# Attention and two quantized convolutions on one core: the instructions in emitted order on every engine, and one kind of single PSUM bank

## The chip, the cores and the metric

The kernel runs on one core of a Trainium2 chip. The metric is the device time of one launch in microseconds: the median of three runs before the change is 3111.85 us (3110.21 to 3114.57). The profiled execution has a span of 3108.4 us, and TensorE was granted a mean clock of 0.981 in it.

In the profile PE is TensorE's matmuls, PEld its weight loads, DVE is VectorE, ACT is ScalarE, POOL is GpSimd, and SP is the engine that here only issues DMAs. Each of them takes its own stream of instructions.

## The reference, cut to what matters

```python
# x: (4, 128, 64, 64); 4 heads of 32 channels; 4096 positions in each image
x_norm = group_norm(x)                                  # 8 groups
q, k, v = split(einsum('oc,bchw->bohw', qkv_w, x_norm) + qkv_b)
attn = softmax(einsum('bhid,bhjd->bhij', q, k) * d ** -0.5)
out  = einsum('bhij,bhjd->bhid', attn, v)
x    = x + einsum('oc,bchw->bohw', proj_w, out) + proj_b
# then, with 3x3 weights quantized to 3 bits:
y = relu(batchnorm(conv3x3(x, wq1)))
y = batchnorm(conv3x3(y, wq2))
return relu(y + x)
```

Attention is most of the work: 4 images x 4 heads x 4096 x 4096 scores, each of which is exponentiated.

## The kernel before: the parts concerned

One **block** is one image and 512 query positions; there are 32 blocks, n = 0 to 31, 8 for each image. A block has 32 **steps**, kt = 0 to 31, one for each 128 key positions. A step needs two **pairs** of score matmuls (two heads each), two exponentials of 128x1024 on ACT, and four matmuls `acc` that weigh the values. The four `acc` matmuls use 32 columns of the array each, so that the four heads stand beside each other; the score matmuls use all 128 columns.

```python
pss = tc.tile_pool(name="pss", bufs=3, space=PSUM)   # 3 x 2 banks: a pair of scores
psa = tc.tile_pool(name="psa", bufs=1, space=PSUM)   # one bank for each kind
ppool = ...bufs=6      # exponentials of one step, 128 x 2048
stage, rpool = ...bufs=1

def scores(pair):                                    # two pairs are one step
    ...
    for i in range(2):
        nc.tensor.matmul(s[:, i, :], k[:, h, c0 : c0 + P], q[:, h, :], ...)
    nc.scalar.activation(pts[step][:, 2 * half : 2 * half + 2, :], s, AF.Exp, scale=SCALE)

def weights(step):
    if kt == 0:
        acc[n] = psa.tile([P, FB], F32, name=f"acc{n}", tag="acc")
    for h in range(HEADS):
        nc.tensor.matmul(acc[n][h * D : (h + 1) * D, :], v[...], pt[:, h, :], ...)
    if kt in MOVED:                # 0, 4, ... 24: this step's sum is made by a DMA that adds
        (kt == 0): nc.sync.dma_start(out=msum[n], in_=pt)
        (else):    nc.gpsimd.dma_start(out=msum[n], in_=pt, accum_op=ALU.add)
    elif kt == 2: nc.vector.tensor_tensor(rsum[n], pts[step - 1], pt, ALU.add)
    elif kt > 2:  nc.vector.tensor_tensor(rsum[n], rsum[n], pt, ALU.add)

run_scores(2)
while at["step"] < steps:
    for s, w in ((3, 1), (3, 2)):      # 3 pairs, 1 step; 3 pairs, 2 steps
        run_scores(s)
        run_weights(w)
```

So scores run two and a half steps ahead of the weighing. The rest of the work is dealt out between: `run_scores` ends with `side("q", kt)` and each step of `run_weights` with `side("a", kt)`, which call what the block's timetable holds up to that step.

```python
add(2, "a", before["total"])          # the previous block's sums: 8 matmuls `l`, then ACT copies to ls
add(4 + j, "", before["invert"](j))   # DVE, four times
add(8, "", before["weigh"]); add(10, "q", before["project"]); add(11, "", before["store"])

def chunk(b, j, kt, fs, loads):       # q, k, v of 512 positions of the next image
    add(kt, "", fs[0])                # ACT: xn <- x
    add(kt, "q", fs[1])               # PE:  pk <- xn
    add(kt + 1, "", fs[2])            # ACT: kh <- pk; DVE: kl <- pk, kh; two DMAs
    add(kt + 1, "q", fs[3])           # PE:  pq <- xn     (pk, pq, pv, l, po: one bank, tag "m")
    add(kt + 2, "", fs[4])            # ACT: qh <- pq; DVE: ql <- pq, qh; two DMAs
    add(kt + 2, "q", fs[5])           # PE:  pv <- xn
    add(kt + 3, "", fs[6])            # DVE: vst <- pv; a DMA
```

Image 0's chunks 3 to 7 are made in block 0. The 8 chunks of each next image are made in the blocks before it: two each in the third and fourth block of an image, one each in the fifth to the eighth. In the last image no chunk is left to make; 8 tasks that quantize the convolution weights on DVE are dealt out there from its second block on.

The convolutions follow, then the last stage:

```python
for b in range(B):
    for j in range(4):
        r = outs.tile([P, Q], F32, tag="r")                      # bufs=4
        nc.sync.dma_start(out=r, in_=y0[b][:, cs])
        y = outs.tile([P, Q], F32, tag="y")                      # bufs=4
        nc.vector.scalar_tensor_tensor(y, cv[b][:, cs], a2, r, ALU.mult, ALU.add)
        nc.scalar.activation(y, y, AF.Relu, bias=c2)
        nc.sync.dma_start(out=out[...][:, cs], in_=y)
```

The code is recorded once, in the order in which it is written; before the change a scheduler then chooses each engine's order from it, and puts one instruction before another where it expects it to be ready sooner.

Of the kernel before, what the change touches and what calls it, by code (L numbers as in the profile page):

```python
# [16 lines left out]
F32 = mybir.dt.float32  # L17
# [3 lines left out]
PSUM = bass.MemoryType.PSUM  # L21

P = 128
# [4 lines left out]
FB = 512  # L28
# [39 lines left out]
def _fast(tc, x, norm_w, norm_b, qkv_wt, qkv_b, proj_wt, proj_b,  # L68
          w1, alpha1, gamma1, beta1, w2, alpha2, gamma2, beta2, out, outer):
    flag = outer.enter_context(tc.tile_pool(name="flag", bufs=1))  # L70
    cnt = flag.tile([1, 1], I32, name="cnt")
    with ExitStack() as ctx:
        _fast_body(ctx, tc, x, norm_w, norm_b, qkv_wt, qkv_b, proj_wt, proj_b,
                   w1, alpha1, gamma1, beta1, w2, alpha2, gamma2, beta2, out, cnt)
    return tc.nc.values_load(cnt[0:1, 0:1], min_val=0, max_val=P)


def _fast_body(ctx, tc, x, norm_w, norm_b, qkv_wt, qkv_b, proj_wt, proj_b,
# [116 lines left out]
    dram = ctx.enter_context(tc.tile_pool(name="dram", bufs=1, space=bass.MemoryType.DRAM))  # L195
    kpool = ctx.enter_context(tc.tile_pool(name="kpool", bufs=NB + 1))
    pss = ctx.enter_context(tc.tile_pool(name="pss", bufs=3, space=PSUM))
    psa = ctx.enter_context(tc.tile_pool(name="psa", bufs=1, space=PSUM))
    y0 = [dram.tile([P, N], F32, name=f"y0_{b}") for b in range(B)]
    att = ExitStack()  # L200
    vpool = att.enter_context(tc.tile_pool(name="vpool", bufs=NB + 1))
# [9 lines left out]
    def f32(t):  # L211
        return t.bitcast(F32)
# [12 lines left out]
    def norm_parts(b, st):  # L225
        mv = small.tile([P, 2], F32, name=f"mv{b}", tag="mv")
        mean = small.tile([P, 1], F32, name=f"mean{b}", tag="mean")
        dv = small.tile([P, 1], F32, name=f"dv{b}", tag="dv")
        gm = {}


        def one():
            nc.vector.bn_aggr(mv, st.rearrange("p j s -> p (j s)"))
            gm[0] = psa.tile([P, FB], F32, name=f"gm{b}", tag="m")
            nc.tensor.matmul(gm[0][:, 0:1], gavg, mv[:, 0:1], start=True, stop=True)

        def two():
            nc.vector.tensor_copy(mean, gm[0][:, 0:1])
            nc.vector.tensor_tensor(dv, mv[:, 0:1], mean, ALU.subtract)
            nc.vector.tensor_tensor(dv, dv, dv, ALU.mult)  # L240
            nc.vector.tensor_tensor(dv, dv, mv[:, 1:2], ALU.add)

        def three():
            gm[1] = psa.tile([P, FB], F32, name=f"gv{b}", tag="m")
            nc.tensor.matmul(gm[1][:, 0:1], gavg, dv, start=True, stop=True)

        def four():
            r = rsqrt_eps(gm[1][:, 0:1], f"gr{b}")
            a = small.tile([P, 1], F32, name=f"ga{b}", tag="ga")
            nc.vector.tensor_tensor(a, r, nw, ALU.mult)  # L250
            c = small.tile([P, 1], F32, name=f"gc{b}", tag="gc")
            nc.vector.tensor_tensor(c, mean, a, ALU.mult)
            nc.vector.tensor_tensor(c, nb, c, ALU.subtract)
            norm[b] = a, c

        return one, two, three, four


# [4 lines left out]
    def project_parts(b, j, xin, wide=False):  # L263
        xn = xpool.tile([P, FB], F32, name=f"xn{b}_{j}", tag="x")
        kq[b, j] = dram.tile([5, P, FB], F32, name=f"kq{b}_{j}")
        ps = {}

        def bank(what):
            if wide:
                t = pss.tile([P, 2, FB], F32, name=f"p{what}{b}_{j}", tag="s")  # L270
                return t[:, 0, :]
            return psa.tile([P, FB], F32, name=f"p{what}{b}_{j}", tag="m")

        def normalize():
            a, c = norm[b]
            nc.scalar.activation(xn, xin(), AF.Identity, bias=c, scale=a)

        def mm(what, o):
            ps[what] = bank(what)
            nc.tensor.matmul(ps[what], wqkv[:, o : o + P], xn, start=True, stop=True)  # L280

        def parts(what, bias, slot):
            hi = stage.tile([P, FB], F32R, name=f"{what}h{b}_{j}", tag=f"{what}h")
            lo = stage.tile([P, FB], F32R, name=f"{what}l{b}_{j}", tag=f"{what}l")
            nc.scalar.activation(hi, ps[what], AF.Identity, bias=bias)  # L285
            nc.vector.scalar_tensor_tensor(lo, ps[what], bias, f32(hi), ALU.add, ALU.subtract)  # L286
            nc.sync.dma_start(out=kq[b, j][slot], in_=f32(hi))
            nc.sync.dma_start(out=kq[b, j][slot + 1], in_=f32(lo))

        def mmv():  # L290
            ps["v"] = bank("v")
            for i in range(KB):
                nc.tensor.matmul(ps["v"][:, i * P : (i + 1) * P], xn[:, i * P : (i + 1) * P],  # L293
                                 wqkv[:, 2 * P : 3 * P], start=True, stop=True)

        def evac_v():
            v = stage.tile([P, FB], F32, name=f"vst{b}_{j}", tag="v")
            nc.vector.tensor_tensor(v.rearrange("p (i f) -> p i f", f=P),
                                    ps["v"].rearrange("p (i f) -> p i f", f=P),
                                    bv.unsqueeze(1).to_broadcast([P, KB, P]), ALU.add)  # L300
            nc.sync.dma_start(out=kq[b, j][4], in_=v)

        return [normalize, lambda: mm("k", P), lambda: parts("k", bk, 0),
                lambda: mm("q", 0), lambda: parts("q", bq, 2), mmv, evac_v]
# [19 lines left out]
    pts, acc, rsum, msum = {}, {}, {}, {}  # L324
# [19 lines left out]
    def weights(step):  # L344
        n, kt = divmod(step, NK)
        v = vs[blocks[n][0], kt // KB]
        pt = pts[step]
        if kt == 0:
            acc[n] = psa.tile([P, FB], F32, name=f"acc{n}", tag="acc")
        for h in range(HEADS):  # L350
            nc.tensor.matmul(acc[n][h * D : (h + 1) * D, :], v[:, kt % KB, h * D : (h + 1) * D],  # L351
                             pt[:, h, :], start=(kt == 0), stop=(kt == NK - 1))
        if kt in MOVED:
            if kt == 0:
                msum[n] = rpool.tile([P, HEADS, FB], F32, name=f"rm{n}", tag="rm")
                nc.sync.dma_start(out=msum[n], in_=pt)
            else:
                nc.gpsimd.dma_start(out=msum[n], in_=pt, accum_op=ALU.add)  # L358
        elif kt == 2:
            rsum[n] = rpool.tile([P, HEADS, FB], F32, name=f"r{n}", tag="r")  # L360
            nc.vector.tensor_tensor(rsum[n], pts[step - 1], pt, ALU.add)  # L361
        elif kt > 2:
            nc.vector.tensor_tensor(rsum[n], rsum[n], pt, ALU.add)  # L363

    def finish_parts(n):

        b, qb = blocks[n]
        av = rpool.tile([P, FB], F32, name=f"av{n}", tag="av")
        rc = rpool.tile([P, FB], F32, name=f"rc{n}", tag="rc")
        t = {}  # L370

        def copy():
            nc.scalar.copy(av, acc[n])


        def total():
            t["l"] = psa.tile([P, FB], F32, name=f"l{n}", tag="m")
            for r in (msum[n], rsum[n]):
                for h in range(HEADS):
                    nc.tensor.matmul(t["l"][h * D : (h + 1) * D, :], ones, r[:, h, :],  # L380
                                     start=(r is msum[n]), stop=(r is rsum[n]))
            t["ls"] = stage.tile([P, FB], F32, name=f"ls{n}", tag="v")
            nc.scalar.copy(t["ls"], t["l"])  # L383

        def invert(j):
            cs = slice(j * P, (j + 1) * P)
            nc.vector.reciprocal(rc[:, cs], t["ls"][:, cs])  # L387

        def weigh():
            nc.vector.tensor_tensor(av, av, rc, ALU.mult)  # L390
            nc.vector.tensor_tensor(worst, worst, t["ls"], ALU.add)
            nc.vector.tensor_tensor(worst, worst, rc, ALU.add)

        def residual():
            t["x"] = load_x(b, qb)

        def project():
            t["o"] = psa.tile([P, FB], F32, name=f"po{n}", tag="m")
            nc.tensor.matmul(t["o"], wp, av, start=True, stop=True)  # L399

        def store():
            nc.vector.scalar_tensor_tensor(t["x"], t["o"], bp, t["x"], ALU.add, ALU.add)
            nc.sync.dma_start(out=y0[b][:, qb * FB : (qb + 1) * FB], in_=t["x"])

        return dict(copy=copy, total=total, invert=invert, weigh=weigh, residual=residual,
                    project=project, store=store)


# [198 lines left out]
    nc.vector.tensor_reduce(big, worst, AX.X, ALU.max)  # L607
    bad = small.tile([P, 1], F32, name="bad")
    nc.vector.tensor_scalar(bad, big, LIMIT, None, ALU.is_gt)
    nbad = psa.tile([P, FB], F32, name="nbad", tag="m")  # L610
    nc.tensor.matmul(nbad[0:1, 0:1], bad, ones[:, 0:1], start=True, stop=True)
    nc.vector.tensor_copy(cnt, nbad[0:1, 0:1])
    att.close()
# [527 lines left out]
```

## Time and profile before

| engine | busy, us | share of the span | instructions |
|---|---|---|---|
| PE | 2967.7 | 95% | 14418 |
| PEld | 1235.4 | 40% | 14418 |
| DVE | 2174.8 | 70% | 1443 |
| ACT | 2130.4 | 69% | 2305 |
| POOL | 189.9 | 6% | 302 |

A matmul on 32-bit data may show as two records (`acc`, `l`, `pk`, `pq`, `pv`, `po`: 8192 records of `acc` are 4096 matmuls); a score matmul shows as one. The ends of matmuls are modelled, so that a PE that is "busy" need not be at its peak: how soon the next run of matmuls of another kind starts says more than the busy time. The attention blocks take the span from about 39 us to 2760 us, the two convolution layers to about 3055 us, and the last stage the rest.

### The profile page before, as it was taken

The page shows a single profiled execution, that of the slowest core. Times are in us where ns is not written, and L with a number is a line of the kernel's source. Part 1 is how long each engine was busy: PE and PEld are TensorE (multiplying, and loading weights), DVE is VectorE, ACT ScalarE, POOL GpSimd, SP SyncE. Part 2 cuts the span into 40 slices and gives each one's busy share as a digit, 9 for nine tenths or more (in the row PEclk, how much of TensorE's full clock was granted, in tenths as well). Part 3 has the DMA queues.
Part 4 walks back from the last instruction along what each step waited for, and adds up shares of the span by engine and source line. Part 5 has one row for each costly group of instructions (what it writes and reads, how often), then busy time and mean ns, then how long its engine had stood idle before and what let it go on. Part 6 is the DMA issues. An engine that isn't in the chain of part 4 may idle for free.

```text
span 3108.4 us, 36462 instructions
## 1 busy us (share of the span) xinstructions
PE 2967.7 (95%) x14418; PEld 1235.4 (40%) x14418; DVE 2174.8 (70%) x1443; ACT 2130.4 (69%) x2305; POOL 189.9 (6%) x302
## 2 busy tenths in 40 slices
PE   6999999998999999989999999999999999999892
PEld 2333333333334433333333433333333333347672
DVE  4577777766877777777787877778787667764333
ACT  4677778776777778767887778767766777731222
POOL 1000000000000000000000000000000000000000
PEclk9999999999999999999999999999999999999996
DMA  8957655577556555596565655785544545442005
GB/s 235 243 109 176 146 136 136 136 167 164 133 110 165 146 131 130 134 206 156 112 163 141 154 124 124 160 195 117 112 104 88 115 99 109 98 100 60 0 1 190
DMA packets 156274, 413.70 MB, mean 133 GB/s; under 512 B 49776, under 2 KB 50544, under 8 KB 127424
## 3 DMA queue, kind: packets, MB, share of 16 engines
q0 software_dynamic: 28128, 201.67, 32.2%
q1 hardware_dynamic: 127392, 208.58, 24.0%
q8 instruction: 115, 1.88, 0.2%
q10 hardware_dynamic: 576, 1.05, 0.1%
q14 instruction: 63, 0.52, 0.1%
HBM read 117.64 MB, written 58.72 MB: 57 GB/s over the span
## 4 chain that ended last, share of the span: by engine, by line
PE 85%; DMA 7%; DVE 2%; ACT 1%; issue 1%; SPq 0%; POOL 0%; POOLq 0%; ACTq 0%; DVEq 0%
PE acc L351 38%; PE s L339 33%; PE c L582 9%; DMA rm<-p 6%; PE l L380 2%; PE po L399 1%; ACT p L340 1%; PE pq L280 1%; PE pv L293 1%; PE pk L280 1%; DVE y L679 1%; DMA r<-y 1%; DVE rc L387 0%; DMA k<-kq 0%; DVE r L363 0%
## 5 line engine op out<-in xcount | busy, mean ns | idle before, releaser
L340 ACT ACTIVATE p<-s 128x1024 f32<-128x1024 f32 x2048 | 1957.7, 1031 | 622.0 <-PE s L339 517.1
L363 DVE TENSOR_TENSOR r<-r,p 128x2048 f32<-128x2048 f32 x736 | 1677.7, 2280 | 174.9 <-ACT p L340 146.5
L351 PE MATMUL acc<-p,v 128*32 128x512 f32 x8192 | 1401.9, 604 | 0.0
L339 PE MATMUL s<-q,k 128*128 128x512 f32 x4096 | 1255.3, 427 | 31.1 <-ACT p L340 22.0
L339 PEld LDWEIGHTS s<-q,k 128*128 128x128 f32 x4096 | 695.5, 189 | 986.0 <-ACT p L340 492.0
L351 PEld LDWEIGHTS acc<-p,v 128*32 128x32 f32 x8192 | 240.6, 108 | 598.0 <-issue 588.6
L358 POOL DMA_DIRECT2D rm<-p x192 | 164.0, 854 | 2480.7 <-ACT p L340 1705.9
L361 DVE TENSOR_TENSOR r<-p,p 128x2048 f32<-128x2048 f32 x32 | 73.4, 2293 | 271.6 <-PE l L380 241.4
L645 ACT COPY cv<-c 128x512 f32<-128x512 f32 x64 | 37.2, 589 | 206.8 <-PE c L582 196.9
L582 PE MATMUL c<-lo,wq 128*128 128x512 f32 x576 | 151.3, 407 | 13.4 <-DVE lo L431 8.2
L582 PE MATMUL c<-hi,wq 128*128 128x512 f32 x576 | 148.3, 401 | 0.0
L582 PEld LDWEIGHTS c<-lo,wq 128*128 128x128 f32 x576 | 107.8, 192 | 48.0 <-ACT cv L645 11.4
L387 DVE RECIPROCAL rc<-ls 128x128 f32<-128x128 f32 x128 | 118.8, 937 | 6.1 <-ACT ls L383 6.1
L582 PEld LDWEIGHTS c<-hi,wq 128*128 128x128 f32 x576 | 108.3, 188 | 29.8 <-issue 0.8
L646 DVE BATCH_NORM_STATS2 st<-cv 128x6 f32<-128x512 f32 x64 | 43.9, 691 | 103.4 <-ACT cv L645 103.4
L286 DVE SCALAR_TENSOR_TENSOR kl<-pk,bk,kh 128x512 fp32r<-128x512 f32 x32 | 24.0, 750 | 127.4 <-ACT kh L285 126.4
L431 DVE TENSOR_TENSOR lo<-t,hi 128x1188 fp32r<-128x1188 f32 x32 | 44.7, 1396 | 39.4 <-PE c L582 35.7
L380 PE MATMUL l<-rm,ones 128*32 128x512 f32 x256 | 64.2, 617 | 4.2 <-DMA rm<-p 4.2
L430 DVE CAST hi<-t 128x1188 fp32r<-128x1188 f32 x32 | 24.9, 778 | 55.4 <-PE c L582 29.8
L380 PE MATMUL l<-r,ones 128*32 128x512 f32 x256 | 52.3, 597 | 2.0 <-DVE r L363 2.0
L399 PE MATMUL po<-av,wp 128*128 128x512 f32 x64 | 37.2, 664 | 16.1 <-DVE av L390 16.1
L383 ACT COPY ls<-l 128x512 f32<-128x512 f32 x32 | 18.8, 587 | 46.2 <-PE l L380 46.0
(99 smaller groups left out, 595.2 us busy)
## 6 DMA issues: line engine op xcount, KB each, us to landing
rm<-p POOLq DMA_DIRECT2D x192, 1024.0 KB, 7.2
k<-kq SPq DMA_DIRECT2D x128, 256.0 KB, 7.0
q<-kq SPq DMA_DIRECT2D x128, 256.0 KB, 4.7
rm<-p SPq DMA_DIRECT2D x32, 1024.0 KB, 5.6
x<-in_x_dram SPq DMA_DIRECT2D x80, 256.0 KB, 4.0
kq<-kh SPq DMA_DIRECT2D x32, 256.0 KB, 5.5
kq<-kl SPq DMA_DIRECT2D x32, 256.0 KB, 6.1
kq<-qh SPq DMA_DIRECT2D x32, 256.0 KB, 4.8
```

Source lines behind the costliest of these rows:

```text
L280: nc.tensor.matmul(ps[what], wqkv[:, o : o + P], xn, start=True, stop=True)
L339: nc.tensor.matmul(s[:, i, :], k[:, h, c0 : c0 + P], q[:, h, :], start=True, stop=True)
L340: nc.scalar.activation(pts[step][:, 2 * half : 2 * half + 2, :], s, AF.Exp, scale=SCALE)
L351: nc.tensor.matmul(acc[n][h * D : (h + 1) * D, :], v[:, kt % KB, h * D : (h + 1) * D], pt[:, h, :], start=(kt == 0), stop=(kt == NK - 1))
L358: nc.gpsimd.dma_start(out=msum[n], in_=pt, accum_op=ALU.add)
L361: nc.vector.tensor_tensor(rsum[n], pts[step - 1], pt, ALU.add)
L363: nc.vector.tensor_tensor(rsum[n], rsum[n], pt, ALU.add)
L380: nc.tensor.matmul(t["l"][h * D : (h + 1) * D, :], ones, r[:, h, :], start=(r is msum[n]), stop=(r is rsum[n]))
L387: nc.vector.reciprocal(rc[:, cs], t["ls"][:, cs])
L399: nc.tensor.matmul(t["o"], wp, av, start=True, stop=True)
L431: nc.vector.tensor_tensor(lo, f32(t), f32(hi), ALU.subtract)
L582: nc.tensor.matmul(ps[:, j, :].rearrange("p (r w) -> p r w", w=W), w[:, tap, :], part[:, j * RB + kh : j * RB + kh + RB, kw : kw + W], sta ...
```

## The change

The whole main path (norm, attention, convolutions, last stage) is put into a region in which each engine issues its instructions in the order in which the code emits them. The scheduler no longer moves any of them. The two kinds of single PSUM bank, `acc` and `m`, become two slots of one kind, so that with a fixed order a new accumulator can take a bank before the old one has been copied out.

```diff
     with ExitStack() as ctx:
+        ctx.enter_context(tc.manual_schedule())
         _fast_body(ctx, tc, x, norm_w, norm_b, qkv_wt, qkv_b, ...
...
-    psa = ctx.enter_context(tc.tile_pool(name="psa", bufs=1, space=PSUM))
+    psa = ctx.enter_context(tc.tile_pool(name="psa", bufs=2, space=PSUM))
...
-            gm[0] = psa.tile([P, FB], F32, name=f"gm{b}", tag="m")
+            gm[0] = psa.tile([P, FB], F32, name=f"gm{b}", tag="a")
...
-            acc[n] = psa.tile([P, FB], F32, name=f"acc{n}", tag="acc")
+            acc[n] = psa.tile([P, FB], F32, name=f"acc{n}", tag="a")
```

Every other tile of tag "m" (`gv`, `pk`, `pq`, `pv`, `l`, `po`, `nbad`) gets the tag "a" in the same way. No operation is added or taken away.

More of the change, by code (lines that the diff above doesn't have):

```diff
@@ L243, in three @@
         def three():
-            gm[1] = psa.tile([P, FB], F32, name=f"gv{b}", tag="m")
+            gm[1] = psa.tile([P, FB], F32, name=f"gv{b}", tag="a")
             nc.tensor.matmul(gm[1][:, 0:1], gavg, dv, start=True, stop=True)
@@ L271, in bank @@
                 return t[:, 0, :]
-            return psa.tile([P, FB], F32, name=f"p{what}{b}_{j}", tag="m")
+            return psa.tile([P, FB], F32, name=f"p{what}{b}_{j}", tag="a")
         def normalize():
@@ L376, in total @@
         def total():
-            t["l"] = psa.tile([P, FB], F32, name=f"l{n}", tag="m")
+            t["l"] = psa.tile([P, FB], F32, name=f"l{n}", tag="a")
             for r in (msum[n], rsum[n]):
@@ L397, in project @@
         def project():
-            t["o"] = psa.tile([P, FB], F32, name=f"po{n}", tag="m")
+            t["o"] = psa.tile([P, FB], F32, name=f"po{n}", tag="a")
             nc.tensor.matmul(t["o"], wp, av, start=True, stop=True)
@@ L609, in _fast_body @@
     nc.vector.tensor_scalar(bad, big, LIMIT, None, ALU.is_gt)
-    nbad = psa.tile([P, FB], F32, name="nbad", tag="m")
+    nbad = psa.tile([P, FB], F32, name="nbad", tag="a")
     nc.tensor.matmul(nbad[0:1, 0:1], bad, ones[:, 0:1], start=True, stop=True)
```

## The prediction

> **What bounds the kernel now.** I read the page first: engine totals, then the costliest groups.
>
> ```profile
> PE 2967.7 (95%) x14418; PEld 1235.4 (40%) x14418; DVE 2174.8 (70%) x1443; ACT 2130.4 (69%) x2305; POOL 189.9 (6%) x302
> ...
> L340 ACT ACTIVATE p<-s 128x1024 f32<-128x1024 f32 x2048 | 1957.7, 1031 | 622.0 <-PE s L339 517.1
> L363 DVE TENSOR_TENSOR r<-r,p 128x2048 f32<-128x2048 f32 x736 | 1677.7, 2280 | 174.9 <-ACT p L340 146.5
> L351 PE MATMUL acc<-p,v 128*32 128x512 f32 x8192 | 1401.9, 604 | 0.0
> ```
>
> PE is the bound: its chain share is 85%, and ACT sits idle 517 us before exponentials because scores come late. But is PE at its best? The chain of waits in one ordinary stretch (start, length, what) tells:
>
> ```profile
> 562.06 1.59 PE s L339 x6
> 563.65 1.00 PE acc L351 x8
> 564.65 1.14 PE s L339 x4
> 565.79 0.97 PE acc L351 x2
> 566.76 0.66 PE s L339 x2
> 567.43 1.85 PE acc L351 x14
> 569.27 1.59 PE s L339 x6
> ```
>
> One matmul of `acc` (x2: two records) costs 0.97 us, four cost 1.00, seven 1.85. So the scheduler, which puts one `acc` matmul between scores, pays nearly a whole run for it, and the six scores that it splits cost 1.14 + 0.66 = 1.80 instead of 1.59. Three steps take 569.27 - 562.06 = 7.21 us. From the trace, the copies of `acc` (L373) end block 0 at 149.8 us and block 31 at 2759.7: 31 blocks, 2610 us. By image (from the end of the block before): blocks 1-8 667, 9-16 671, 17-24 663, 25-31 609.
>
> The second place is the last stage, in the timeline:
>
> ```profile
> 3075.07 4.98 ACT L680 ACTIVATE y<-y,bc 128x1024 f32<-128x1024 f32 x4 [7.49 <-DVE y L679]
> 3076.24 4.17 SPq L681 DMA_DIRECT2D out_dram<-y  x4
> 3080.50 2.25 SPq L677 DMA_DIRECT2D r<-y  x4
> 3085.37 5.12 DVE L679 SCALAR_TENSOR_TENSOR y<-cv,ba,r 128x1024 f32<-128x1024 f32 x4 [6.51 <-DMA r<-y]
> ```
>
> The scheduler issues loads and stores in fours: four quarters every 11.6 us (3073.75 to 3085.37 for DVE), so that one load's latency is paid once in four.
>
> [...] `acc` uses 32 columns and `s` 128, and the visit of a single `acc` matmul costs 0.97 us. [...] So a fixed order is kept, with whatever wait stands at the head; the trace before has such waits (DVE stood 241.4 us before L361, the first add of a block, waiting for `l`). [...] Here three pairs of score banks are what couples PE to ACT.
>
> **The change part by part.** Nothing is added; I compared the order of the two built kernels on each engine.
>
> (a) *Ordinary triples.* Before: 1058 runs of `acc` matmuls on PE, 338 of them of one or two matmuls. After: 693, of 4, 8 or (once) 12, and 681 runs of six scores. A triple is then s6 + acc4 + s6 + acc8 = 1.58 + 1.00 + 1.58 + 1.85 = 6.01 us. ACT needs 6 exponentials at a cadence of 0.94 us (six in 5.65 in the timeline), 5.64 us. With three score buffers PE waits some 0.2 for the third exponential: 6.2 against 7.21. A block has 32/3 triples: 66.2 us. Added to it: `l` 1.85, `po` 0.95, and a wait of some 2.1 us: `rm` of step 0 can start only after `l` (about 7.9 us into the block), its DMA takes 5.6, and the seventh exponential tile needs that slot (6 slots). A block without a chunk: 71.1 us. Before, these are 76 to 80 in the middle images and 80 to 96 in the last one.
>
> (b) *Chunks.* In emitted order `xn`, `kh` and `qh` stand on ACT right behind the three exponentials of the scores just issued, and `pk`, `pq`, `pv` stand on PE right behind those scores; in each of the 24 chunks after block 0, two of the three matmuls have no slack at all. After six scores (1.5 us) PE must wait for ACT: first exponential at 0.82, three end at 3.65, then `xn` 0.81: about 4.5, a wait of 3.0. For `pq` (the bank is free only after `kl`): 3.65 + `kh` 0.69 + `kl` 0.75 + 0.2 for the handing over = 5.2, a wait of 3.2 to 3.7. Together 6.6 us a chunk, and the three matmuls' own 2.8 (0.95 + 0.95 + 0.9). One-chunk block: 71.1 + 9.4 = 80.5; two-chunk: 89.9. Before: 78 to 83 and 84 to 86. **This eats the gain of (a) wherever there are chunks.**
>
> (c) *Blocks by image.* First of an image (DMA loads of the last keys, `rm` at 12 us instead of 7): 77. Second: 73 (group norm's two matmuls wait for DVE). Two with two chunks: 179.8. Three with one: 241.5. Last (all keys of the next image are loaded; before, DMA busy 0.87 of it): 86.5. Sum for blocks 1-8: 657.8, three times 1973, against 2000: -27.
>
> (d) *The last image.* Block 25 gets five of six weight-quantizing tasks, 6.1 us of DVE each (13 instructions), with DVE at 61 of 71 us already: 100. Block 26: 74. Four at 71.1 = 284, block 31: 74. Sum 532 against 609: -77. The scheduler cut `acc` finest here: 48 and 49 runs in blocks 26 and 27 (94 and 96 us), some 31 elsewhere; 21 or 22 after.
>
> (e) *Block 0 and the convolutions.* Block 0: 66 + five chunks at 9.4 = 113 against 111 us (first exponential 39.0 to 149.8): +3, rounded up. Convolutions: PE runs them back to back at 0.234 us before and after; -4 for the splitting around `l` at 2757 to 2790 us.
>
> (f) *The last stage.* Emitted: load r, store y, load r, store y, all on SP. A store waits for ACT, and the next load stands behind it. One quarter is then: load 4.5 (alone 4.28; first of four behind stores 4.80), DVE 0.08 + 1.28, to ACT 0.04, ACT 1.17, store to next load 0.43: 7.5 us. From the first store at 3060.7: 15 x 7.5 = 112.5, so the last store at 3173, then 5.0 to the end (landing 3.2 and 1.8, as before): 3178 against 3108: **+70**.
>
> Sum: -27 - 77 + 3 - 4 + 70 = -35; 3112 - 35 = 3077, rounded to 3075 us.
>
> **The rivals.** *R1: the waits of (b) are hidden*, because ACT runs ahead or PE would have waited anyway. For it: PE waits of (a) overlap some. Against: with six scores in 1.5 us and three exponentials in 2.8, PE reaches `pq` first. Without (b) the 24 chunks give 24 x 6.6 = 158 us back: about 2915. *R2: in-order DVE becomes the bound.* DVE has 23 adds at 2.37 (four in 9.47), 3.4 of reciprocals, 2.8 for weigh and store, 2.2 of a chunk: 61 to 66 of 71 us, and it stands still some 6 us at the start of each block until `l` is there. For it: 241 us of exactly that wait before. Against: six exponential slots let it lag three steps. Some 3 us more in 25 blocks: 3150. *R3: the DMAs that add up `rm` bound the blocks* (7 in a chain, 6.9 each at least, up to 13.8 at an image's end). Blocks of 71 us leave 8.9 for four steps; only if contention raises the DMAs past that does the chain lengthen: +40. *R4: the tail is hidden*, if a load alone behind one store is faster or the last stage starts earlier: it cannot, since r and y stand in one queue; at best -15.
>
> **Range and chances.** The gain of (a) and the loss of (f) are read from durations and I trust them to 30 and 8 us. (b) may be wrong by half, 80 us, either way; R2 and R3 only add. I take 3000 to 3140 for 8 in 10. Faster by over 2% means below 3049.6: chance 0.34. Slower by over 2%, above 3174: 0.08. Within: 0.58.
>
> **What would show it.** (a): runs of `acc` of 8 and 16 records, none of 2; triples of about 6.2 us in a block without chunks, 71 us from copy to copy. (b): PE idle or weight loads waiting before L281 and L294, named after ACT xn, DVE kl or ql, some 150 us in all; `acc` copies 80 and 90 us apart in chunk blocks. (d): block 25 with DVE at nearly full time. (f): SP alternating r and out every 7.5 us, and a last stage of about 120 us instead of 49. Blocks with chunks at 72 us would prove R1; DVE near its full time in ordinary blocks R2; PE waiting at `l` for DMA R3.

## The result and the profile after

| kernel | median, us | range | ratio to before, 95% interval |
|---|---|---|---|
| before | 3111.45 | 3110.21 to 3114.57 | 1 |
| changed | 3259.11 | 3255.49 to 3263.38 | 1.0474 [1.0455, 1.0492] |

The change makes the kernel 4.7% slower; the prediction was 3075 us. The page of the changed kernel (totals, clock, the chain by engine and by line, groups), in the same parts as before:

```profile
PE 2738.6 (84%) x14418; PEld 1227.0 (38%) x14418; DVE 2197.1 (68%) x1443; ACT 2099.2 (65%) x2305; POOL 184.2 (6%) x302
...
PEclk8899999988999899988999999989999999999975
...
PE 52%; DMA 25%; ACT 7%; DVE 6%; issue 5%; SPq 0%; ACTq 0%; POOLq 0%; DVEq 0%; POOL 0%
...
L341 ACT ACTIVATE p<-s 128x1024 f32<-128x1024 f32 x2048 | 1927.3, 1038 | 670.9 <-PE s L340 411.9
...
L352 PE MATMUL acc<-p,v 128*32 128x512 f32 x8192 | 1090.1, 636 | 0.0
...
L281 PE MATMUL pk<-xn,wqkv 128*128 128x512 f32 x64 | 50.0, 875 | 80.7 <-ACT xn L277 80.7
```

The chain by engine in the kernel before:

```profile
PE 85%; DMA 7%; DVE 2%; ACT 1%; issue 1%; SPq 0%; POOL 0%; POOLq 0%; ACTq 0%; DVEq 0%
```

PE is busy for 229 us less (2967.7 before), and `acc` alone for 312 less (1401.9 before; the groups overlap in time, so that their figures do not add up to PE's). That is the intended gain. But PE's share of the chain fell from 85% to 52%, and DMA's rose from 7% to 25%: PE is no longer the only bound. Before exponentials ACT waits less for scores (411.9 against 517.1) and yet is idle longer in all (670.9 against 622.0), so it waits for something else. The list of waits (engine and operation, what it waited for; us in total, times, longest) names it, first in the changed kernel:

```profile
ACT p L341 <- DMA rm<-p: 216.9, 75, 10.1
...
PE pk L281 <- ACT xn L277: 80.7, 22, 7.6
...
PE pq L281 <- DVE kl L287: 57.6, 19, 4.6
PE pv L294 <- DVE ql L287: 54.7, 20, 3.4
```

and in the kernel before:

```profile
ACT p L340 <- DMA rm<-p: 62.1, 30, 5.7
```

Exponentials wait for a free slot of `p`, which an adding DMA of `rm` (the tile of the sum that the code calls `msum`) still reads, 155 us longer than before. The three matmuls of a chunk wait 193 us where before they waited 6; 165 of the 193 lie in blocks 1 to 31. The chain of the changed kernel (start, length, what) shows an ordinary triple and then the end of image 0:

```profile
665.58 1.75 PE s L340 x6
667.34 1.85 PE acc L352 x16
669.19 1.59 PE s L340 x6
670.78 0.99 PE acc L352 x8
671.78 1.75 PE s L340 x6
...
684.93 2.86 ACT p L341 x3
...
687.86 13.53 DMA rm<-p
...
701.91 13.29 DMA rm<-p
...
715.74 11.74 DMA rm<-p
...
753.87 9.80 DMA k<-kq
763.68 14.17 DMA q<-kq
```

A triple is 671.78 - 665.58 = 6.20 us, as predicted; the median of the 444 plain triples in blocks 1 to 31 is 6.21. But as soon as the next image's keys are loaded, the chain passes to DMA, 12 to 14 us for an addition, and then to the loads of `k` and `q` themselves.

Where the time went, by stage (ends of the copies of `acc` in the trace, us; the last stage counts from the start of the last batch norm's aggregation on DVE):

| kernel | block 0 ends | blocks 1-8, 9-16, 17-24 | 25-31 | convolutions | last stage |
|---|---|---|---|---|---|
| before | 149.8 | 667, 671, 663 | 609 | 295.9 | 52.9 |
| changed | 157.7 | 702, 709, 705 | 535 | 318.6 | 126.6 |

Mean length of a block by its kind, us (copy of `acc` to copy of `acc`):

| kernel | first of an image | second | two chunks | one chunk | last of an image | 27-30 |
|---|---|---|---|---|---|---|
| predicted | 77 | 73 | 89.9 | 80.5 | 86.5 | 71 |
| changed | 76.9 | 78.0 | 94.9 | 84.5 | 107.1 | 72.3 |
| SP by the scheduler (`not_sp`) | 76.2 | 73.4 | 92.0 | 81.1 | 98.1 | 69.6 |
| PE alone in order (`pe_only`) | 76.4 | 75.7 | 79.7 | 77.6 | 93.0 | 69.5 |
| `q` behind `rm` (`q_pool`) | 75.3 | 77.4 | 91.7 | 82.4 | 106.3 | 70.5 |
| before | 89.5 | 78.1 | 83.7 | 80.8 | 89.4 | 86.3 |

### The profile page after: what moved, and what is told of

Its sections match the earlier page's. It is cut to its first block, busy times and chain, and to the rows that moved or that the text cites. A ratio compares the mean times of both kernels' runs of the same rounds, so it can differ in the third digit from the quotient of the medians.

```text
span 3253.5 us, 36390 instructions
## 1 busy us (share of the span) xinstructions
PE 2738.6 (84%) x14418; PEld 1227.0 (38%) x14418; DVE 2197.1 (68%) x1443; ACT 2099.2 (65%) x2305; POOL 184.2 (6%) x302
## 4 chain that ended last, share of the span: by engine, by line
PE 52%; DMA 25%; ACT 7%; DVE 6%; issue 5%; SPq 0%; ACTq 0%; POOLq 0%; DVEq 0%; POOL 0%
DMA rm<-p 20%; PE s L340 20%; PE acc L352 19%; PE c L583 7%; ACT p L341 5%; DVE r L364 3%; DMA r<-y 2%; PE l L381 2%; PE pk L281 1%; DMA q<-kq 1%; PE pv L294 1%; PE pq L281 1%; DMA k<-kq 1%; DVE y L680 1%; ACT y L681 1%
## 5 line engine op out<-in xcount | busy, mean ns | idle before, releaser
L341 ACT ACTIVATE p<-s 128x1024 f32<-128x1024 f32 x2048 | 1927.3, 1038 | 670.9 <-PE s L340 411.9
L352 PE MATMUL acc<-p,v 128*32 128x512 f32 x8192 | 1090.1, 636 | 0.0
L340 PEld LDWEIGHTS s<-q,k 128*128 128x128 f32 x4096 | 713.7, 194 | 976.6 <-ACT p L341 514.9
L352 PEld LDWEIGHTS acc<-p,v 128*32 128x32 f32 x8192 | 203.8, 112 | 518.4 <-issue 508.6
L583 PE MATMUL c<-lo,wq 128*128 128x512 f32 x576 | 153.9, 412 | 28.5 <-ACT cv L646 20.5
L281 PE MATMUL pk<-xn,wqkv 128*128 128x512 f32 x64 | 50.0, 875 | 80.7 <-ACT xn L277 80.7
L287 DVE SCALAR_TENSOR_TENSOR ql<-pq,bq,qh 128x512 fp32r<-128x512 f32 x32 | 24.0, 749 | 118.9 <-ACT qh L286 118.8
L281 PE MATMUL pq<-xn,wqkv 128*128 128x512 f32 x64 | 44.0, 776 | 57.6 <-DVE kl L287 57.6
L680 DVE SCALAR_TENSOR_TENSOR y<-cv,ba,r 128x1024 f32<-128x1024 f32 x16 | 20.5, 1283 | 97.2 <-DMA r<-y 97.2
L294 PE MATMUL pv<-wqkv,xn 128*128 128x128 f32 x256 | 39.6, 302 | 54.7 <-DVE ql L287 54.7
L681 ACT ACTIVATE y<-y,bc 128x1024 f32<-128x1024 f32 x16 | 18.4, 1147 | 104.1 <-DVE y L680 104.1
```

What stands on the lines that cost most here:

```text
L583: nc.tensor.matmul(ps[:, j, :].rearrange("p (r w) -> p r w", w=W), w[:, tap, :], part[:, j * RB + kh : j * RB + kh + RB, kw : kw + W], sta ...
```

## The experiments

My theory after the result: PE's fixed order is worth what (a) and (d) said; the fixed order of the other engines gives it back in three places, that of ACT (and of DVE behind it) in the chunks, SP's in the last stage, and SP's again inside the blocks, which I had counted as nothing. The rivals: the shared banks cost; the halved TensorE clock costs.

### Taking the change apart

Each of these restricts the region to some engines, or leaves the region out. The diffs are against the changed kernel and in short form; in `pe_old_banks` the two kinds of bank are those of before as well.

```diff
 psum_only     -        ctx.enter_context(tc.manual_schedule())
 pe_only       +        ctx.enter_context(tc.manual_schedule(engines={PE}))
 pe_old_banks  +        ctx.enter_context(tc.manual_schedule(engines={PE}))   # banks as before
 sp_only       +        ctx.enter_context(tc.manual_schedule(engines={SP}))
 not_sp        +        ctx.enter_context(tc.manual_schedule(engines={PE, DVE, ACT, POOL}))
```

**psum_only.**

> The two PSUM banks as one kind of two slots, no region of emitted order: the scheduler orders all engines as before. Theory: the order makes the whole difference and the banks none, so 3112 us, within 15. Rival: the shared banks themselves cost (pk, pq, pv and l now compete with acc for a bank), which would show here as 3150 or more.

Measured 3154.0 us, 1.0137 [1.0119, 1.0156]. The rival was right: under the scheduler the shared banks cost 43 us; they do not help by themselves.

**pe_only.**

> Emitted order for PE alone: runs of 4 and 8 acc matmuls as in the changed kernel, while the scheduler places ACT, DVE, POOL and SP. Theory: the clean runs are the gain, and most of the waits before pk, pq and pv come from ACT's and DVE's fixed order, so this keeps the gain without most of the loss: about 2980, and in any case below 3112. Rival: the waits belong to PE's fixed order alone (no other matmul can fill them), so that they stay whatever ACT does, about 140 us of them: 3110 to 3150.

Measured 2947.49 us, 0.948 [0.9453, 0.9506]: the whole of the change but the order of the other four engines, and 312 us faster than it. The theory was right, with 33 us more gain than it expected.

**pe_old_banks.**

> Emitted order for PE alone, with the two banks kept as two kinds (acc and m, one each), to be set beside 2947 us with them as two slots of one kind. Theory: with a fixed order on PE the shared slots let a new accumulator start before the old one is copied, 32 times a wait of about 0.6 us or less, so the old banks cost 0 to 20 us: 2947 to 2967. Rival: the shared slots cost what they cost under the scheduler (43 us), as l and the chunk's matmuls wait for the accumulator's copy: then this is about 2905.

Measured 2966.25 us, 0.9528 [0.9512, 0.9545]. With PE in order, the shared banks bring 19 us. Their sign depends on the order, as the change had supposed.

**sp_only.**

> Emitted order for SP alone, which here issues DMAs and nothing else; PE, ACT and DVE stay with the scheduler. Theory: the order of the DMA issues costs 74 us in the last stage (load and store one by one) and some 15 us at each of three images' ends, where the next image's q stands last behind all key loads: about 3225. Rival: at the images' ends the loss came from PE, ACT and DVE, whose order is not fixed here; then only the last stage shows: 3186.

Measured 3332.35 us, 1.0711 [1.0694, 1.0729]. Both figures were far too low. SP's order alone is worse than the whole change: the first block of an image takes 113.3 us (89.5 before). PE three times stands before a score matmul for a load of `q`, 73.9 us together and 26.5 at most. Against `psum_only`, which has the same banks, SP's order costs 178 us.

**not_sp.**

> Emitted order for PE, DVE, ACT and POOL, while the scheduler places the DMA issues of SP. Theory: the last stage falls back to about 53 us (-74) and the three blocks at the images' ends from 107 to about 90 (-50): about 3135. Rival: the images' ends stay at 107, since the keys' DMAs are as slow as before: 3185. The waits before pk, pq and pv, some 140 us, and the waits in the convolutions stay in either case.

Measured 3081.51 us, 0.9895 [0.9879, 0.9912]: 53 us below even the theory, which looked for SP's cost only in the last stage and at the images' ends.

So there is a ladder: 3111.5 us before; PE in order 2966.3 (-145); shared banks 2947.5 (-19); ACT, DVE and POOL in order 3081.5 (+134); SP in order 3259.1 (+178). SP's step is as large when SP alone is in order (`sp_only`), so it does not hang on the order of the ladder. In the traces it is 101 us in blocks 1 to 31 (2650.6 against 2549.3) and 73 in the last stage. The third step, of ACT, DVE and POOL, was not divided further; 26 us of it are block 25, where DVE's tasks for the convolution weights now stand in line (94.8 us in `not_sp`, 68.8 in `pe_only`).

### The last stage and the convolutions

**ends.** Loads of `r` are issued three quarters ahead, and a band's two copies come after the matmuls of both halves, as does the preparation of a later band. The diff is in short form.

```diff
+    for _ in range(3):
+        ahead()                     # loads the next quarter's r
...
-            r = outs.tile(...); nc.sync.dma_start(out=r, in_=y0[b][:, cs])
+            r = fetched.pop(0)
+            ahead()
...
-            for j in range(2): conv(j); copy(j)
+            for j in range(2): conv(j)
+            for j in range(2): copy(j)
```

> The changed kernel with two stretches of its emitted order rewritten: in the last stage the load of r is emitted three quarters ahead of its use, and in a convolution band both halves are emitted before the two copies out of PSUM. Theory: the last stage returns from 126.6 to about 53 us, and the convolutions from 318.6 to about 296, since PE no longer waits some 0.7 to 1.1 us in each band for ACT's copy of the first half: 3259 - 73 - 23 = 3163. Rival for the convolutions: the 1.1 us is the wait for the activation that makes the next band, not for the copy; then they stay at 318.

Measured 3151.2 us, 1.0124 [1.0084, 1.0164]. The last stage fell from 126.6 to 46.5 us, the convolutions from 318.6 to 290.2, and blocks 1 to 31 stayed (2655 against 2651): the theory was right, and its rival for the convolutions fell. The last stage of the changed kernel, in its timeline, is what (f) worked out:

```profile
3132.16 0.35 SPq L682 DMA_DIRECT2D out_dram<-y  x1
3132.56 0.43 SPq L678 DMA_DIRECT2D r<-y  x1
3137.09 1.28 DVE L680 SCALAR_TENSOR_TENSOR y<-cv,ba,r 128x1024 f32<-128x1024 f32 x1 [6.13 <-DMA r<-y]
3138.41 1.15 ACT L681 ACTIVATE y<-y,bc 128x1024 f32<-128x1024 f32 x1 [6.27 <-DVE y L680]
3139.58 0.34 SPq L682 DMA_DIRECT2D out_dram<-y  x1
```

One load, DVE, ACT, one store, and only then the next load: 7.42 us here. In the convolutions the timeline of the changed kernel shows a wait that I had not seen:

```profile
3051.05 2.31 PE L583 MATMUL c<-hi,wq 128*128 128x512 f32 x9
...
3053.46 0.58 ACT L646 COPY cv<-c 128x512 f32<-128x512 f32 x1 [2.52 <-PE c L583]
...
3054.09 1.97 PEld L583 LDWEIGHTS c<-lo,wq 128*128 128x128 f32 x9 [1.17 <-ACT cv L646]
3054.10 2.42 PE L583 MATMUL c<-lo,wq 128*128 128x512 f32 x9 [0.73 <-ACT cv L646]
```

Half of a band's matmuls end, ACT copies the result out, and the next matmuls stand behind that copy; 30 times 0.7 us (20.5 in all), and the run behind it takes 2.42 us where the run before it took 2.31. In `ends` this wait is gone. Before the change the scheduler had mixed the matmuls of two halves (runs of 13, 9, 5 and 9 in PE's timeline), and PE stood so only 4 times, 5.2 us in all.

### The chunks and the clock

**chunk.** The seven parts of a chunk are spread over seven steps, so that `xn`, `kh` and `qh` are asked for a step ahead of the matmul that needs them. Numbers are steps from the chunk's first.

```diff
-            0: xn, pk   1: kh, pq   2: qh, pv   3: vst
+            0: xn   1: pk   2: kh   3: pq   4: qh   5: pv   6: vst
```

> The changed kernel with each chunk after block 0 dealt out over seven steps instead of four, so that three pairs of scores stand between each operation of ACT (xn, kh, qh) and the matmul that needs it (pk, pq, pv). Theory: PE's waits before these matmuls, 166 us with those of block 0, fall to some 35, and with them most of the windows of half clock [...]: 3259 - 130 - 70 = about 3060; one-chunk blocks at 75 us. Rival: PE would have waited for exponentials anyway, the wait only moves to the scores: 3200 or more.

Measured 3084.67 us, 0.9912 [0.9894, 0.9929], 174 us less than the changed kernel, which is nearer the theory; the rival fell. `pk`, `pq` and `pv` now wait 11, 12 and 19 us in all (81, 58 and 55 in the changed kernel); a block with two chunks takes 79.7 us, with one 76.7. So a chunk's waits cost (94.9 - 79.7) / 2 = 7.6 and 84.5 - 76.7 = 7.8 us, with all that follows from them. In the last blocks of images, where DMA rules (`rm`, `q` and `k` are 58% of the chain of block 7 in the changed kernel), the same edit brings only 4.5 us (107.1 to 102.6).

Behind many of these waits the clock granted to TensorE is halved, in 62 windows in blocks 1 to 31. In PE's timeline of the changed kernel:

```profile
538.55 1.83 PE L340 MATMUL s<-q,k 128*128 128x512 f32 x6
545.77 2.07 PE L281 MATMUL pk<-xn,wqkv 128*128 128x512 f32 x2 [5.40 <-ACT xn L277]
547.77 3.64 PE L352 MATMUL acc<-p,v 128*32 128x512 f32 x16
551.35 1.85 PE L340 MATMUL s<-q,k 128*128 128x512 f32 x6
553.04 1.02 PE L281 MATMUL pq<-xn,wqkv 128*128 128x512 f32 x2
```

After 5.40 us of idleness `pk` takes 2.07 us, where `pq`, a matmul of the same shape, takes 1.02 at 553.04, and the next run of `acc` 3.64 instead of the 1.92 that this timeline shows for other runs of 16 records. The granted clock from 545.7 to 552.0 is 0.52. The prediction had left this out. In blocks 1 to 31 a window of half clock begins in an idle gap of PE, or within 2 us of its end, with 38 of 42 gaps of 3 us or more and with 17 of 25 of 2.5 to 3 us. In all 335 us of blocks 1 to 31 are at half clock (38 before). But does it cost time by itself?

**warm.** Eight needless matmuls before each `pk` behind block 0's first three, whose results are overwritten.

```diff
+            if what == "k" and not wide:
+                for _ in range(8):
+                    nc.tensor.matmul(ps[what][:, : 3 * P], wqkv[:, o : o + P], wqkv, ...)
```

> The changed kernel with 8 needless matmuls (128x384, into the same bank, overwritten by pk) before pk in each chunk after the first three: PE works through its wait for xn and does nothing useful. Theory: it is not the wait alone that costs but the halved TensorE clock [...]; with PE kept busy 16 or so of these windows vanish, so the kernel with more work is faster: about 3215, with the half-clock time of the attention stage down from 335 us to some 230. Rival: the clock does not matter, since ACT is what PE waits for: 3260 to 3290, slower by the part of the extra matmuls that lies beyond the wait.

Measured 3278.03 us, 1.0529 [1.051, 1.0547]: slower, with half clock down to 242 us. But the matmuls also stood where `pk` had slack, and block 0 alone became 12.6 us longer (170.3; at most 166 in the other runs).

**warm16.** Six of them, only in the 16 chunks whose `pk` has no slack.

```diff
+            if what == "k" and (b, j) in COLD:      # 16 chunks
+                for _ in range(6):
+                    nc.tensor.matmul(ps[what][:, : 3 * P], wqkv[:, o : o + P], wqkv, ...)
```

> The changed kernel, with six needless 128x384 matmuls ahead of the pk matmuls of the 16 chunks whose pk has no slack (none in block 0, none in chunks that have slack). Theory that the halved clock after a wait of PE costs time by itself: the windows of half clock behind pk go, and with them about 2 us a chunk, so about 3225 us. Rival, that ACT's queue bounds the stretch after a wait and PE at half clock still keeps up: the half-clock time falls and the time stays at 3250 to 3265 us.

Measured 3243.64 us, 1.0428 [1.0411, 1.0445]. It lies between the two: 15 us less, for 72 us less of half clock (263). The halved clock costs something, about a fifth of its windows, and is not the main cause of the miss. The spread chunks bring 174 us because they take the waits away; half clock falls there too, from 335 to 184 us, which at a fifth would be some 30 of the 174 (an estimate).

### SP's order inside the blocks

In the changed kernel SP issues the next block's `q` right behind `rm` at the start of the block. The timelines of SP and of POOL there, in block 28:

```profile
2527.97 0.47 SPq L357 DMA_DIRECT2D rm<-p  x1
2528.49 3.80 SPq L309 DMA_DIRECT2D q<-kq  x4
```

```profile
2534.22 0.85 POOL L359 DMA_DIRECT2D rm<-p  x1 [29.89 <-ACT p L341]
2543.63 0.84 POOL L359 DMA_DIRECT2D rm<-p  x1 [8.56 <-DMA rm<-p]
```

From the first adding DMA to the next it takes 9.4 us: the first is issued while the four loads are under way (the last of them lands at 2538.7) and lands at 2543.1. Until then it holds a slot of `p`, and an exponential that needs it must stand. The page's list of DMAs (KB each, median us to landing) had the clue before the change:

```profile
q<-kq SPq DMA_DIRECT2D x128, 256.0 KB, 4.7
```

and has this after it:

```profile
q<-kq SPq DMA_DIRECT2D x128, 256.0 KB, 7.1
```

The scheduler had issued most of `q` 70 to 90 us into a block, behind the sums: of the 128 loads, 35 overlap a DMA of `rm`. Emitted order issues most of it at 6 to 10 us, and 124 of 128 overlap one. The additions, which POOL issues, slow down beside SP's loads: 9.4 us from one to the next here, 7.6 without them in `q_pool` below. Four runs move these loads.

**loadq.** `q` at step 11 instead of step 2.

```diff
-            add(2, "", lambda: load_q(b, qb + 1))
+            add(11, "", lambda: load_q(b, qb + 1))
```

> The changed kernel with the next block's q loaded at step 11 instead of step 2, so that its four DMAs no longer stand right in front of the first adding DMA of rm. Theory: that DMA (issued at step 4) falls from 9 to 10 us to 7, ACT's waits for rm from 217 us to about 130, and each of 28 blocks gives 2 to 3 us: about 3190. Rival: the load delays the later adding DMAs by as much, and nothing is won: 3250 to 3265.

Measured 3308.25 us, 1.0635 [1.0616, 1.0654]: worse than the rival. The first adding DMA takes 7.0 us from issue to landing again in most blocks (9 to 10 in the changed kernel), but the one at step 16 takes 10 to 13 in more than half of them, and the chunk's load of `x` now stands behind `q` on SP: ACT's wait for `x` before `xn` grew from 2 to 53 us, and PE's idle time before `pk` in blocks 1 to 31 from 69 to 105.

**q_early.** The next image's first `q` at step 3 of the last block instead of step 26.

```diff
-            add(26, "", lambda: load_q(b + 1, 0))
+            add(3, "", lambda: load_q(b + 1, 0))
```

> The changed kernel with one line altered: in the last block of an image the next image's first q is issued at step 3 instead of step 26, where it stands behind all loads of the next image's keys. Theory: PE's wait of some 24 us for this q at the end of these three blocks is the step that the prediction left out, and it goes: the blocks fall from 107 to some 90 us, so 3259 - 45 = about 3214. Rival: q lands in time, but the keys behind it come as much later, and the next image's first block waits for them instead: 3250 to 3260.

Measured 3234.93 us, 1.0396 [1.0379, 1.0414], between theory and rival. In the trace the last blocks of images fell by 2.1 us only and the first ones by 3.4; the wait moved to `k`, `v` and `rm`. So the place of this `q` is worth 24 us and not 45.

**q_spread.** One DMA of `q` at each of steps 18, 20, 22 and 24 (diff in short form).

```diff
-            add(2, "", lambda: load_q(b, qb + 1))
+            for s in range(4): add(18 + 2 * s, "", part(s))
```

> The changed kernel, with the next block's q loaded by one DMA at each of steps 18, 20, 22 and 24, instead of four together at step 2. Theory that SP's order costs because q's four loads stand right before the adding DMA of rm at step 4: that DMA falls from 9 to 10 us to about 7 us, loads late in the block do no harm, and the time is about 3200 us. Rival, that the loads cost the same wherever they stand (they hold back another rm or the chunk's x): 3255 us or more.

Measured 3226.12 us (3212.98 to 3235.09), 1.0381 [1.0363, 1.04], between theory and rival. The first adding DMA is at 7.0 us in most blocks, but the one at step 16 or 20 takes 9 to 14 where SP reaches the loads just then.

**q_pool.** `q` is issued by GpSimd, behind the block's last adding DMA.

```diff
-            add(2, "", lambda: load_q(b, qb + 1))
+            add(26, "", lambda: load_q(b, qb + 1, nc.gpsimd))
```

> The changed kernel, with the next block's q issued by GpSimd behind the last adding DMA of rm, at step 26, instead of by SP at step 2. So the four loads come after the chain of rm, at the end of the block, where the scheduler had them in the kernel before and in the kernel whose SP it orders. Theory that the place of q is the greater part of what SP's fixed order costs in blocks without loads of a whole image: all adding DMAs of a chain take about 7 us, blocks with two chunks come down from 94.9 to 92, with one from 84.5 to 81, the second of an image from 78 to 74, the last image's from 72.3 to 70, and the time is about 3195 us. Rival, that q only has to leave step 4, and the rest of SP's cost has another cause: the same as with q spread over steps 18 to 24, 3215 to 3235 us. Third: q now lands too late for the next block's first scores, and the time is 3250 us or more.

Measured 3208.12 us, 1.0302 [1.0285, 1.0319], 51 us less than the changed kernel and 13 short of the theory. In POOL's timeline of this kernel the loads come behind the last addition of a block, and the next block's first one takes 7.6 us to the next:

```profile
2535.90 0.85 POOL L359 DMA_DIRECT2D rm<-p  x1 [8.33 <-ACT p L341]
2536.44 2.55 POOL L309 DMA_DIRECT2D q<-kq  x4
2564.65 0.92 POOL L359 DMA_DIRECT2D rm<-p  x1 [25.66 <-DMA rm<-p]
2572.22 0.85 POOL L359 DMA_DIRECT2D rm<-p  x1 [6.65 <-DMA rm<-p]
```

Blocks with chunks and those of the last image are at the lengths of `not_sp`, or near (table above). So the place of `q`, with the engine that issues it (the edit changes both), is about half of SP's 101 us: blocks 1 to 31 take 2597.6 us, 53 less. The rest stands in the last blocks of images (106.3 against 98.1, three times) and the second ones (77.4 against 73.4), where SP also loads keys, values and `x`. Which of these loads costs there was not tried, and stays open.

### Together

**all_mended.** Every engine in order, with the edits of `ends`, `chunk` and `q_early`.

```diff
+ the edits of ends, chunk and q_early
```

> The full region of the changed kernel with all the repairs: loads of r three quarters ahead, copies after both halves, chunks over seven steps, the next image's q early. Theory: the four losses are apart from each other and add up: 3259 - 108 (last stage and convolutions) - 174 (chunks) - 45 (q) = 2932, so that a fixed order on every engine is as good as one on PE alone. Rival: SP's fixed order has further costs in each block (the adding DMA of rm behind the loads of q), and ACT's waits for rm grow as the rest gets faster: 2990.

Measured 2927.16 us, 0.9402 [0.9386, 0.9419]. That the sum comes out within 5 us is in part luck: its last term was measured as 24 and not 45, and the three measured gains add up to 2953. The parts together bring 26 us more than apart; why was not tried.

**pe_spread.** PE alone in order, with the spread chunks and the copies behind both halves.

```diff
-        ctx.enter_context(tc.manual_schedule())
+        ctx.enter_context(tc.manual_schedule(engines={PE}))
+ the edit of chunk, and the convolutions' part of ends
```

> Emitted order for PE alone, with the chunks spread over seven steps and the copies of both halves of a convolution band after both halves. Theory: the two largest waits that a fixed order on PE leaves are these, some 70 us before pq and pv and some 30 in the convolutions (325 us against 296): 2947 - 60 - 30 = about 2860, the fastest so far. Rival: the scheduler places ACT and DVE for the old spacing and the waits move to the scores, as half of them may: 2920.

Measured 2846.22 us, 0.9133 [0.9106, 0.9159]: the fastest. Its page, in the parts shown above:

```profile
PE 2632.1 (93%) x14418; PEld 1210.4 (43%) x14418; DVE 2166.5 (76%) x1443; ACT 2095.3 (74%) x2305; POOL 186.2 (7%) x302
...
PE 60%; DMA 17%; DVE 10%; ACT 4%; issue 3%; SPq 0%; DVEq 0%; ACTq 0%; POOLq 0%; POOL 0%
```

PE is busy 93% of the span again, with 336 us less to do than before. A fixed order on every engine, with the repairs above, is 81 us behind.

## Why the prediction was wrong, step by step

Predicted -35, measured +148 (medians); the stages of the two traces give +145.

| step | predicted | measured | what the runs showed |
|---|---|---|---|
| (a) triples | 6.2 us, block 71.1 | 6.20, blocks 27-30 72.3 | right |
| (b) chunk waits | 6.6 us a chunk, 158 in all | PE idle 165 in all; 7.6 to 7.8 a chunk by `chunk` | mechanism right; the wait itself 6.9, the rest not traced (half clock may be part of it) |
| (c) blocks 1-24 | -27 | +115 | failed: SP's order, ends of images |
| (d) last image | -77 | -74 | right in sum, in part by luck: block 25 95 for 100, block 26 82 for 74, block 31 69 for 74 |
| (e) block 0, convolutions | +3, -4 | +8, +23 | failed for the convolutions: PE stands behind ACT's copy (`ends`); block 0's rest not traced |
| (f) last stage | +70 | +74 | right |

**The step that failed** is (c), with R3 beside it. The prediction counted SP's fixed order only in (f), and in the blocks as nothing; it took over the DMA times of the kernel before ("7 in a chain, 6.9 each at least") and allowed +40 if contention raised them. Yet the change moves exactly those loads: `load_q` stands at step 2 in the timetable, next to `rm`, where the scheduler had not left it. In the runs SP's order in blocks 1 to 31 is worth 101 us (`not_sp`), about half of it by the place of `q` (`q_pool`). R3 was the right rival, and 2.5 times larger than written; it showed not at `l`, where the prediction looked for it, but in exponentials that wait for a slot of `p` (216.9 us).

The 142 us by which (c) was short divide by blocks: last of an image 3 x 20.6 = 62, one chunk 9 x 4.0 = 36, two chunks 6 x 5.0 = 30, second 3 x 5.0 = 15. Without SP's order (`not_sp`) blocks 1 to 24 take 2025 us, so 90 of the 142 go with it; 35 of the other 52 lie in the last blocks of images. The 86.5 us for these had a second fault: it let PE's gain shorten a block in which DMA rules. The chain of block 7 before the change is 64% additions of `rm`. No kernel here has them below 89 us in the mean, neither the one before (89.4) nor the fastest (90.9).

One reading behind (a) was wrong, though its sum came out. The prediction set the 0.97 us of a lone `acc` matmul beside the 32 columns of `acc` and the 128 of `s`, as if the change from the one to the other made it dear. Its own figures say otherwise: four `acc` matmuls cost 1.00 and eight 1.85, so that the part of a visit that does not grow is 1.00 - (1.85 - 1.00) = 0.15 us; for the scores (six 1.59, four 1.14, two 0.66) it is some 0.2. Both are estimates from the chain before the change, and what a change of columns costs could only be in these parts. A lone matmul is dear because the same 0.97 us would have held all four heads. `pq`, which uses all 128 columns, takes 1.06 in the chain of the kernel before. Two of its sums are 0.1 us off (66.1 for 66.2 and 5.3 for 5.2), which changes nothing.

**The other rivals.** R1 fell: the waits of (b) are in the list of waits in full, and `chunk`, which takes them away, is 174 us faster. R2 fell for ordinary blocks: with DVE in order and SP not, blocks 27 to 30 take 69.6 us (`not_sp`), with PE alone in order 69.5 (`pe_only`). It holds in block 25, as (d) said: DVE is busy 85.1 of its 95.1 us. R4 fell: a quarter takes 7.4 to 8.3 us.

(b) is for the most part a step of the order of ACT and DVE (not tried apart), not of PE's: with PE alone in order the scheduler puts `xn` at least 24 exponentials earlier in all 24 chunks and `kh` three earlier in 13, PE's waits in blocks 1 to 31 fall from 165 to 70 us, and a block with two chunks takes 79.7 us with the timetable unchanged (`pe_only`). The prediction said that a fixed order is kept, "with whatever wait stands at the head", and drew the conclusion for ACT and the last stage, not for SP's loads in between.

## What to carry to other kernels

Fix the order of the engine whose order is the trouble, here PE's, and leave the others to the scheduler, or write the code for a fixed order first: results asked for a step ahead, loads several stores ahead, copies behind both halves. When an order becomes fixed, go through the queue of every issuing engine and ask where the scheduler had put each transfer; the list of DMAs with its times to landing shows which had been moved out of the way. Two transfers that never met before have not shown what they cost each other.

## What the runs showed of the hardware that I had not expected

- Half clock came after idle gaps of PE: after 38 of 42 of 3 us or more, 17 of 25 of 2.5 to 3 us and 5 of 10 of 2 to 2.5 (blocks 1 to 31 of the changed kernel). Its windows last 3.4 us (28 of 62), 6.8 (32) or 10.2 (2).
- Filling such gaps with needless matmuls brings little: 15 us for 72 us of half clock (`warm16`), and it costs where the gap wasn't there (`warm`).
- An adding DMA of 1 MB takes 7.0 us from issue to landing in most blocks when the loads of `q` do not run beside it (`q_pool`), 9 to 10 beside these four loads of 256 KB (8.9 at 2534.22 in the changed kernel), and 11.4 to 14.2 while a next image's keys are loaded (five of the six in each of blocks 7, 15 and 23; 7.0 for the other).
- The shared banks cost 43 us under the scheduler and bring 19 with PE in order.
